# Softplus of two scan chunks at once: the dt of one chunk five units sooner, of the other eight

## The chip, the cores and the metric

The kernel runs on one core of a Trainium2 chip. The metric is the device time of one execution in microseconds (us). The engines are PE (TensorE, matrix products; PEld is its weight load), DVE (VectorE), ACT (ScalarE, activation functions), POOL (GpSimd) and SP (SyncE, which here does nothing but issue transfers between memory and the chip, one after the other). All of them work from lists of instructions in program order and wait for one another by semaphores.

## The reference

The input x has 4 images of 48 x 48 positions and 128 channels. Layer 0 adds a state-space block to it; layer 1 adds attention and then a spectral convolution. Cut to what matters here:

```python
# layer 0, per image: K=4 orders of the L=2304 positions, d=256 channels, N=16 states
xs = stack([x0, x1, x0[..., ::-1], x1[..., ::-1]])        # rows, columns, both backwards
x_dbl = einsum('bkdl,kcd->bkcl', xs, x_proj_w)
dts_r, Bs, Cs = x_dbl[:, :, :8], x_dbl[:, :, 8:24], x_dbl[:, :, 24:]
dt = softplus(einsum('bkrl,kdr->bkdl', dts_r, dt_proj_w) + dt_proj_b)
A = -exp(A_logs)
for l in range(L):                                        # a scan along the positions
    h = h * exp(dt[l] * A) + (dt[l] * xs[l]) * B[l]
    ys[l] = sum_n(h * C[l])
x = x + out_proj(layernorm(ys of the 4 orders added) * silu(z))
# layer 1
t = t + softmax(ln(t) ln(t)^T) ln(t)
t = t + spectral_convolution(ln(t))                       # 16 filters, long causal convolutions
```

The two functions of ACT that this document is about are in it: softplus makes dt, and exp(dt A) makes the decay of every state at every position.

## The kernel before

The four images (batches) are worked off in a pipeline. For each batch b there are two stages: the scans of b, with the spectral convolution of batch b - 1 laid between their instructions (in batch 0 a mixing of filters, `mixture`), and then the epilogue and attention of b, with the input projection of batch b + 1 laid between. After the last batch the last convolution runs alone.

**Chunks and units.** A scan is cut into chunks of CS = 384 positions: 4 orders x 6 chunks = 24 chunks a batch, 96 in all (`order`, which lists them by k and c). A chunk's 256 channels and 16 states make 8 units (`quads`: h is the half of the channels, q a quarter of the states), and a unit has four scans of 128 x 384 (L510, on DVE). So a batch has 192 units. Before its scans a unit needs dt x B (L494, on DVE for five units of eight, on POOL for three), and for each scan a decay, exp(A dt), made by ACT (L503). After them POOL multiplies by C (L520) and PE sums over the states (L528).

**The ring.** The decays go to PSUM tiles, a `Ring` of 5 in batch 0 and 4 after it. `fill` has ACT make decays as long as a tile is free, so ACT runs ahead of DVE by what the ring holds. Two other things borrow tiles of the ring: a copy of B for the units that DVE enters (`spread`, L486), and the products of the next chunks' preparation (`mm_hold`).

**Preparation of a chunk.** `Chunk.prep` is a generator that `prepare` calls three times per unit; three calls are a step. It takes 15 steps (`STEPS`) and begins 17 units (`LEAD`) before the chunk's first unit, so two or three chunks are prepared at a time. For k < 2 PE projects x (L407) and ACT writes the result to a tile xd (L412), which SP stores to `xdd` in memory; for k >= 2 SP loads xd from there (L398). Then, for each half h, PE makes dt (L421) and ACT copies it to `re` (L424). ACT applies Softplus to both halves at once (L433). DVE makes dt x (L451), SP stores dt and dt x of each half to memory (L440), and loads them back replicated over partitions as `rep` (L445), four transfers per half. `rep` is what the decays and the units read.

**B and C.** `fetch` (L472) broadcasts rows of `xdd` to the tiles `bc0` to `bc7`, four transfers of SP per tile. In the scans the tiles are fetched again one by one, as they come free. For the first chunk of a batch `begin_scans` fetches all eight, 32 transfers.

**The start of a batch's scans.** `begin_scans` is a generator too. For batch 0 it runs at one go behind the input projection. For the others it is called once per step of attention over its last 23 steps (`BEGIN`); a step of attention is one product for the scores (L811), one Exp on ACT (L813) and one product with the values (L803). It prepares chunk 0 in full, fetches its B and C, and carries chunk 1 through 27 calls. Attention's own work of a step, its tail for a finished block among it (`tail`, whose loads and stores go to SP as well: `tu<-td`, `ud<-uT` at L1052, `td<-T` at L1019), comes in the lists ahead of what `begin_scans` adds in that step. After the last step the scans begin, and with them the convolution `stu`, whose first instructions fetch its table tiles `tt` (L1110).

**The convolution.** `stu` has 5 blocks of output rows x 16 filters = 80 items. An item is three sets of products on PE (L1151), whose results ACT copies (L1167, L1171, L1174, L1175), and a projection (L1214). At a block's first item `begin` loads its inputs, among them the residual `res` (L1187), which `ended` adds to the result one or two items after the block's last.

Of the kernel before, what the change touches and what calls it, by code (L numbers as in the profile page):

```python
# [8 lines left out]
F32 = mybir.dt.float32  # L9
AF = mybir.ActivationFunctionType  # L10
# [49 lines left out]
def hybrid_kernel(ctx: ExitStack, tc: tile.TileContext, a: dict, out: bass.AP):  # L60
# [304 lines left out]
    class Chunk:  # L365


        def __init__(self, b, k, c):
            self.b, self.k, self.lo = b, k, c * CS
            self.name = f"{b}_{k}_{c}"  # L370
            self.bc, self.rep = {}, []
            self.rev = k >= 2
            self.first = c == (NCH - 1 if self.rev else 0)
            self.last = c == (0 if self.rev else NCH - 1)

            self.slot = CS if self.rev else 0
            self.at = slice(0, CS) if self.rev else slice(1, CS + 1)

        def prep(self, pool):

            k, name, xc = self.k, self.name, xcs[self.b]
            xdd_ = xdd[k % 2][self.lo // CS]

            def rest(n=1):

                yield  # L390
                yield 0
                yield
                for i in range(3 * n - 3):
                    yield 0 if i % 3 == 1 else None

            if k >= 2:
# [12 lines left out]
            yield 2 * CS if k < 2 else 0  # L409
            yield  # L410
            if k < 2:
                nc.scalar.activation(xd, ps[:, :CS], AF.Identity, bias=onerow)  # L412
                mm_done(hold)
            yield from rest()

            re = pool.one.tile([P, NH, 2, CS], F32, tag="re", name=f"re{name}")
            for h in range(NH):
                hold = mm_hold()
                yield
                ps = mm_tile(f"dt{name}_{h}", hold)  # L420
                nc.tensor.matmul(ps[:, :CS], dtw[:, k, h * P:(h + 1) * P], xd, start=True, stop=True)  # L421
                yield CS
                yield
                nc.scalar.copy(re[:, h, 0], ps[:, :CS])  # L424
                mm_done(hold)
                if h == 0:
                    if k < 2:
                        nc.sync.dma_start(xdd_, xd)
                    yield from rest()
            yield  # L430
            yield 0

            nc.scalar.activation(re[:, :, 0], re[:, :, 0], AF.Softplus)  # L433
            yield
            yield
            yield 0
            d = dram.tile([NH, G4, DL, 2, CS], F32, tag="dtdu", name=f"dtdud{name}")

            def store(h):
                nc.sync.dma_start(d[h].rearrange("g j i t -> (g j) i t"), re[:, h])  # L440

            def load(h):
                rep = pool.rep.tile([P, G4, 2, CS], F32, tag="rep", name=f"rep{name}_{h}")
                for c in range(C4):
                    nc.sync.dma_start(rep[c::C4], d[h].rearrange("g j i t -> j g i t"))  # L445
                self.rep.append(rep)

            for h in range(NH):
                x = in_order(xc[h], k, self.lo, CS)
                dt, dx = [re[:, h, i].rearrange("p (r w) -> p r w", w=x.shape[2]) for i in range(2)]  # L450
                nc.vector.tensor_tensor(dx, dt, x, ALU.mult)  # L451
# [12 lines left out]
            yield  # L464
# [78 lines left out]
    POOLED = ((0, 3), (1, 1), (1, 3))  # L543
    order = [(k, c) for k in range(K) for c in (range(NCH) if k < 2 else reversed(range(NCH)))]
    quads = [(h, q) for h in range(NH) for q in range(Q4)]
    STEPS = 15
    LEAD = 17
    FETCHED = range(2 * Q4)

    CHUNK_COLS = len(quads) * CS + 3 * CS  # L550

    def begin_scans(b, pool):

        chunks = [Chunk(b, k, c) for k, c in order]
        preps = [ch.prep(pool) for ch in chunks]
        for i in range(7):
            next(preps[0])
        for i in range(3 * STEPS - 7):
            if next(preps[0]) is not None:
                yield  # L560
        for i in FETCHED:
            chunks[0].fetch(i, pool)
        for i in range(3 * (LEAD - len(quads))):
            if next(preps[1]) is not None:
                yield
        for i in range(3 * (LEAD - 2 * len(quads))):
            next(preps[2])
        yield chunks, preps

    def scans(b, chunks, preps, front, sp, back, ring, finish, work, work_cols):  # L570
# [39 lines left out]
        def prepare(s):  # L610

            ci, j = divmod(s, len(quads))
            for c in range(ci + 1, ci + 4):
                if c < len(chunks) and 0 <= s - len(quads) * c + LEAD < STEPS:
                    done[0] += next(preps[c]) or 0

        def refill(s, i):
# [439 lines left out]
    def stu(b, pool, ps, seeds):  # L1057
# [119 lines left out]
        def begin(n):  # L1177
            (lo, hi, place, extra), k = items[n]
            m = 2 if extra else 1

            now["x"] = pool.one.tile([P, 6, P], F32, tag="ux", name=f"ux{b}_{n}")
            nc.sync.dma_start(now["x"][:, 2:, :hi - lo], ud[:, :, 1 + lo:1 + hi])
            nc.sync.dma_start(now["x"][:, :2, :hi - lo], ud[:, 2:, lo:hi])
            now["mu"] = pool.one.tile([P, 2, 3, C], F32, tag="mue", name=f"mue{b}_{n}")
            nc.sync.dma_start(now["mu"][:, :m], mud[:, place:place + m])
            now["T", n] = pool.two.tile([P, 4, C], F32, tag="res", name=f"res{b}_{n}")
            nc.sync.dma_start(now["T", n][:hi - lo], td[4 * lo:4 * hi].rearrange("(p j) c -> p j c", j=4))  # L1187

        def parts(w, extra):
# [56 lines left out]
        for n, (_, k) in enumerate(items):  # L1246
            if k == 0:
                begin(n)
            yield from conv(n, 0)
            if n > 0:  # L1250
                fetch_G(n - 1)
# [279 lines left out]
    run(prologue(0, turn.one, mm_tile), 3, weights(once.one))  # L1531
    turn.close()
    once.close()
    front = Stage(tc, "f0", "left", one=(1, SB), xd=(3, SB), rep=(3, SB))
    first = begun(begin_scans(0, front))
    begin0.close()
    start_y(0)
    for b in range(B):
# [48 lines left out]
                parts.pop(0)()  # L1587
        if more:
            turn.close()
            front = Stage(tc, f"f{b + 1}", "left", one=(1, SB), xd=(3, SB), rep=(3, SB))  # L1590
            start_y(b + 1)
            pieces = begin_scans(b + 1, front)
        first = None
# [81 lines left out]
```

## Time and profile before

| | |
|---|---|
| time, median of 3 runs | 5618.99 us (5607.94 to 5623.74) |
| the profiled execution, its own time | 5605.93 us |
| span of its instructions | 5604.2 us |
| mean granted clock of TensorE | 0.931 |
| scans of batches 0 to 3, first to last scan | 951.4, 1006.6, 1006.6, 1000.0 us |
| what follows the last scan (attention of batch 3, then the last convolution alone) | 788.1 us |

The profile is of one execution. A line of its groups has the line of the kernel, the engine, the operation, the tiles (written <- read), shapes, the count, then busy time, the mean of one in ns, and the idle time of the engine before it. In a timeline a line has the start from the span's start, the length, the engine (SPq is SP's queue of transfers), and in brackets the idle time before it with what ended it. Neighbouring instructions of one kind on one engine are merged, with their count.

### The profile page before, as it was taken

To read this page: it belongs to the slowest core of one execution; us is meant where nothing else is said; L and a number is where in the kernel's file an instruction comes from. 1 tells how busy PE (TensorE), PEld (TensorE's weight loads), DVE (VectorE), ACT (ScalarE), POOL (GpSimd) and SP (SyncE) were. 2 spreads that over 40 slices of the span, in tenths; PEclk is the share of its full clock that TensorE was granted. 3 is DMA by queue.
4 is the path that set the end of the run, shared out by engine and by line. 5 is a ranking of instruction groups with operands and counts; after the bars stand their busy time and mean duration, and the time that the engine had idled before them with its cause. 6 is when DMAs were issued, how large, how long until landed. Compare 5 with 4: busy or idle time off the path is not lost. (4 is left out here: it accounts for less than half of the span.)

```text
span 5604.2 us, 74073 instructions
## 1 busy us (share of the span) xinstructions
PE 4809.4 (86%) x23582; PEld 3073.9 (55%) x23582; DVE 4344.4 (78%) x5307; ACT 3324.7 (59%) x6923; POOL 3661.9 (65%) x1882
## 2 busy tenths in 40 slices
PE   3556556688999998898999998898999999889999
PEld 1211111345556666645566666645666667659987
DVE  6999999855899999756999999656999999523211
ACT  2777777546777776446777776446777766432111
POOL 1899999614889998505888998505888998301100
PEclk6877777799999999999999999999999999999999
DMA  3545545306777778416777878417887778226543
GB/s 104 164 150 169 168 158 168 102 30 180 234 239 251 257 252 266 158 33 200 229 245 244 262 242 280 133 39 206 240 249 251 256 249 281 92 63 158 143 146 94
DMA packets 741422, 1035.17 MB, mean 185 GB/s; under 512 B 142760, under 2 KB 564904, under 8 KB 740968
## 3 DMA queue, kind: packets, MB, share of 16 engines
q1 hardware_dynamic: 735208, 1027.13, 58.5%
q10 hardware_dynamic: 5824, 3.30, 0.3%
q8 instruction: 189, 3.10, 0.2%
q14 instruction: 201, 1.65, 0.1%
HBM read 911.77 MB, written 118.31 MB: 184 GB/s over the span
## 5 line engine op out<-in xcount | busy, mean ns | idle before, releaser
L510 DVE TENSOR_TENSOR_SCAN s<-ring,s 128x385 f32<-128x385 f32 x3072 | 2702.3, 940 | 130.9 <-ACT ring L503 129.8
L520 POOL TENSOR_TENSOR s<-s,bc 128x1536 f32<-128x1536 f32 x764 | 2426.6, 3178 | 127.6 <-DVE s L510 62.7
L503 ACT ACTIVATE ring<-rep,A 128x384 f32<-128x384 f32 x3072 | 1758.6, 584 | 784.5 <-DVE s L494 458.1
L494 POOL TENSOR_TENSOR s<-rep,bc 128x1536 f32<-128x1536 f32 x288 | 994.2, 3452 | 162.5 <-DMA bc<-xdd 161.6
L494 DVE TENSOR_TENSOR s<-rep,ring 128x1536 f32<-128x1536 f32 x480 | 832.0, 1734 | 92.3 <-ACT ring L486 40.9
L528 PE MATMUL y<-s,csum 128*32 128x384 f32 x6144 | 712.0, 538 | 184.0 <-POOL s L520 111.6
L1151 PE MATMUL cx<-tt,us 128*128 128x252 f32 (+7 forms) x2880 | 630.3, 359 | 92.7 <-ACT U L1175 55.5
L1151 PE MATMUL cx<-tt,u 128*128 128x252 f32 (+7 forms) x2880 | 620.9, 356 | 63.4 <-ACT cy L1167 62.1
L1151 PE MATMUL cy<-tt,u 128*128 128x252 f32 (+5 forms) x2880 | 611.6, 354 | 31.0 <-DMA tt<-fd 31.0
L1151 PEld LDWEIGHTS cx<-tt,us 128*128 128x128 f32 x2880 | 484.1, 193 | 273.4 <-issue 88.4
L1151 PEld LDWEIGHTS cx<-tt,u 128*128 128x128 f32 x2880 | 479.8, 192 | 275.2 <-ACT cy L1167 101.5
L1151 PEld LDWEIGHTS cy<-tt,u 128*128 128x128 f32 x2880 | 488.3, 194 | 165.6 <-issue 116.0
L1214 PE MATMUL pr<-U,G 128*128 128x288 f32 (+6 forms) x1536 | 451.2, 423 | 11.6 <-DMA G<-gd 11.5
L528 PEld LDWEIGHTS y<-s,csum 128*32 128x32 f32 x6144 | 126.4, 111 | 544.7 <-issue 273.2
L1468 POOL TENSOR_TENSOR t<-s,s 128x512 f32<-128x512 f32 x48 | 63.7, 1326 | 541.1 <-ACT s L1466 541.1
L813 ACT ACTIVATE e<-s,shift 128x512 f32<-128x512 f32 (+1 forms) x360 | 230.9, 644 | 290.7 <-PE s L811 290.3
L931 PE MATMUL G<-M,W 128*128 128x256 f32 (+3 forms) x512 | 234.9, 574 | 192.1 <-ACT W L921 83.4
L811 PE MATMUL s<-xnT 128*128 128x512 f32 (+1 forms) x720 | 341.3, 559 | 13.3 <-ACT xnT L771 13.3
L803 PE MATMUL o<-e,xn 128*128 128x512 f32 (+1 forms) x720 | 337.4, 552 | 2.1 <-ACT e L813 2.1
L518 POOL COPY carry<-s 128x4 f32<-128x4 f32 x640 | 121.2, 189 | 323.8 <-DVE s L510 288.0
L1214 PEld LDWEIGHTS pr<-U,G 128*128 128x128 f32 x1536 | 256.1, 192 | 138.1 <-issue 81.4
L931 PEld LDWEIGHTS G<-M,W 128*128 128x128 f32 x512 | 102.9, 233 | 320.3 <-issue 131.4
(236 smaller groups left out, 5203.6 us busy)
## 6 DMA issues: line engine op xcount, KB each, us to landing
rep<-dtdud SPq DMA_DIRECT2D x768, 384.0 KB
bc<-xdd SPq DMA_DIRECT2D x3072, 48.0 KB
tt<-fd SPq DMA_DIRECT2D x144, 577.0 KB
dtdud<-re SPq DMA_DIRECT2D x192, 384.0 KB
tt<-fd SPq DMA_DIRECT2D x144, 505.0 KB
tt<-fd SPq DMA_DIRECT2D x144, 379.0 KB
G<-gd SPq DMA_DIRECT2D x160, 256.0 KB
t<-fd SPq DMA_DIRECT2D x80, 384.0 KB
```

Source lines behind the costliest of these rows:

```text
L494: eng.tensor_tensor(s, self.ch.rep[self.h][:, :, 1], bt.unsqueeze(1).to_broadcast([P, G4, CS]), ALU.mult)
L503: nc.scalar.activation(ring.body(self.dA[g]), ch.rep[self.h][:, g, 0], AF.Exp, scale=A[:, ch.k, self.h * G4 + g, self.q:self.q + 1])
L510: nc.vector.tensor_tensor_scan(s, ring.decays(i, ch.rev), s, 0.0, ALU.mult, ALU.add)
L518: nc.gpsimd.tensor_copy(carry[:, self.h, self.q].unsqueeze(2), self.s[:, :, end:end + 1])
L520: eng.tensor_tensor(self.s, self.s, ch.bc[Q4 + self.q].unsqueeze(1).to_broadcast([P, G4, CS]), ALU.mult)
L528: nc.tensor.matmul(ch.y[g * DL:(g + 1) * DL, :CS], csum, self.s[:, g], start=(self.q == 0), stop=(self.q == Q4 - 1))
L803: nc.tensor.matmul(po[J][:, :w], xn[:, i], e[:, :w], start=(i == 0), stop=(i == NT - 1))
L811: nc.tensor.matmul(p[:, :w], xnT[:, i * P:(i + 1) * P], xnT[:, 512 * J:512 * J + w], start=True, stop=True)
L813: nc.scalar.activation(e[:, :w], p[:, :w], AF.Exp, bias=shift)
L931: nc.tensor.matmul(p[:, :n], W[:, q if t else 0, i], M[t][:, i].unsqueeze(1).to_broadcast([P, n, C]), start=(t == 0 and i == 0), stop=(t = ...
L1151: nc.tensor.matmul(p4[:, 1:3, v - (hi - at):] if g else p4[:, 0:4:3, v - (hi - at):], x, t[:, :, hi - 1 - at + J * P:end if end >= 0 else ...
L1214: nc.tensor.matmul(o if q else o.rearrange("p f r m -> p r f m"), G, U[n][:, 4 * q:4 * q + 4, v0:v1].rearrange("p (a b) m -> p a b m", a=2 ...
```

## The change

The preparation of even and odd chunks (by their place in `order`) gets different lengths. An even chunk begins 5 units sooner and waits 5 steps between its copies of dt and its Softplus, so that its Softplus stays where it was. An odd chunk begins 8 units sooner and waits 8 steps behind its Softplus, so that everything from dt x on stays where it was. The Softplus of chunk c + 1 thereby comes in the same call of `prepare` as that of chunk c, right behind it. As dt now lives longer, `re` becomes three tiles: `dt0` and `dt1` for even and odd chunks, and `dx` for dt x; a half of a chunk is stored with two transfers in place of one. To make room, `xd` has two buffers in place of three, and the residual of the convolution one in place of two; it is loaded at the second to last item of its block. `begin_scans` prepares chunks 0 and 1 side by side up to their Softplus, then the rest of chunk 0 together with the first 18 calls of chunk 2, and then fetches B and C.

```diff
+            self.odd = i % 2
...
-            re = pool.one.tile([P, NH, 2, CS], F32, tag="re", name=f"re{name}")
+            dt = pool.one.tile([P, NH, CS], F32, tag=f"dt{self.odd}", name=f"dt{name}")
...
-            nc.scalar.activation(re[:, :, 0], re[:, :, 0], AF.Softplus)
+            if not self.odd:
+                yield from rest(EARLY)
+            nc.scalar.activation(dt, dt, AF.Softplus)
+            if self.odd:
+                yield from rest(len(quads))
             yield
             yield
             yield 0
+            dx = pool.one.tile([P, NH, CS], F32, tag="dx", name=f"dx{name}")
...
             def store(h):
-                nc.sync.dma_start(d[h].rearrange("g j i t -> (g j) i t"), re[:, h])
+                for i, x in enumerate((dt, dx)):
+                    nc.sync.dma_start(d[h].rearrange("g j i t -> (g j) i t")[:, i], x[:, h])
...
-    STEPS = 15
-    LEAD = 17
+    EARLY = 5
+    STEPS = (15 + EARLY, 15 + len(quads))
+    LEAD = (17 + EARLY, 17 + len(quads))
...
-        for i in range(7):
-            next(preps[0])
-        for i in range(3 * STEPS - 7):
-            if next(preps[0]) is not None:
+        calls = [0] * len(preps)
+
+        def go(c, n):
+            for i in range(calls[c], n):
+                next(preps[c])
+            calls[c] = n
+
+        DT = 23
+        for i in range(8, DT + 4):
+            go(0, min(i, DT))
+            go(1, i - 3)
+            if i % 3 != 0:
+                yield
+        go(0, DT + 3 * EARLY)
+        go(0, DT + 3 * EARLY + 1)
+        go(1, DT + 1)
+        ends = [3 * (LEAD[c % 2] - len(quads) * c) for c in range(4)]
+        ends[0] = 3 * STEPS[0]
+        yield
+        for i in range(DT + 3 * EARLY + 2, ends[0] + 1):
+            go(0, i)
+            go(2, min(i - DT - 3 * EARLY, ends[2]))
+            if i % 3 == 0:
                 yield
         for i in FETCHED:
             chunks[0].fetch(i, pool)
-        for i in range(3 * (LEAD - len(quads))):
-            if next(preps[1]) is not None:
-                yield
-        for i in range(3 * (LEAD - 2 * len(quads))):
-            next(preps[2])
+        for c in range(1, 4):
+            go(c, ends[c])
         yield chunks, preps
...
-            for c in range(ci + 1, ci + 4):
-                if c < len(chunks) and 0 <= s - len(quads) * c + LEAD < STEPS:
+            for c in range(ci + 1, ci + 5):
+                if c < len(chunks) and 0 <= s - len(quads) * c + LEAD[c % 2] < STEPS[c % 2]:
                     done[0] += next(preps[c]) or 0
...
-            now["T", n] = pool.two.tile([P, 4, C], F32, tag="res", name=f"res{b}_{n}")
+
+        def residual(n):
+            (lo, hi, place, extra), k = items[n]
+            now["T", n] = pool.one.tile([P, 4, C], F32, tag="res", name=f"res{b}_{n}")
...
+            if k == KF - 2:
+                residual(n - k)
...
-    front = Stage(tc, "f0", "left", one=(1, SB), xd=(3, SB), rep=(3, SB))
+    front = Stage(tc, "f0", "left", one=(1, SB), xd=(2, SB), rep=(3, SB))
```

The last edit stands a second time, for the batches after the first.

More of the change, by code (lines that the diff above doesn't have):

```diff
@@ L365, in hybrid_kernel, with __init__ @@
     class Chunk:
-        def __init__(self, b, k, c):
+        def __init__(self, b, i, k, c):
             self.b, self.k, self.lo = b, k, c * CS
+            self.odd = i % 2
             self.name = f"{b}_{k}_{c}"
@@ L423, in prep @@
                 yield
-                nc.scalar.copy(re[:, h, 0], ps[:, :CS])
+                nc.scalar.copy(dt[:, h], ps[:, :CS])
                 mm_done(hold)
@@ L449, in prep @@
                 x = in_order(xc[h], k, self.lo, CS)
-                dt, dx = [re[:, h, i].rearrange("p (r w) -> p r w", w=x.shape[2]) for i in range(2)]
-                nc.vector.tensor_tensor(dx, dt, x, ALU.mult)
+                v, o = [y[:, h].rearrange("p (r w) -> p r w", w=x.shape[2]) for y in (dt, dx)]
+                nc.vector.tensor_tensor(o, v, x, ALU.mult)
             yield
@@ L552, in begin_scans @@
     def begin_scans(b, pool):
-        chunks = [Chunk(b, k, c) for k, c in order]
+        chunks = [Chunk(b, i, k, c) for i, (k, c) in enumerate(order)]
         preps = [ch.prep(pool) for ch in chunks]
-        for i in range(7):
-            next(preps[0])
-        for i in range(3 * STEPS - 7):
-            if next(preps[0]) is not None:
+        calls = [0] * len(preps)
[19 more added lines that the diff above has]
+            if i % 3 == 0:
                 yield
@@ L1589, in hybrid_kernel @@
             turn.close()
-            front = Stage(tc, f"f{b + 1}", "left", one=(1, SB), xd=(3, SB), rep=(3, SB))
+            front = Stage(tc, f"f{b + 1}", "left", one=(1, SB), xd=(2, SB), rep=(3, SB))
             start_y(b + 1)
```

## The prediction

> **What bounds the kernel now.** I read the page's first part first (busy time of each engine, share of the span, instructions):
>
> ```profile
> PE 4809.4 (86%) x23582; PEld 3073.9 (55%) x23582; DVE 4344.4 (78%) x5307; ACT 3324.7 (59%) x6923; POOL 3661.9 (65%) x1882
> ```
>
> ACT, whose work the change regroups, is the least busy of the five. The change lives in the scans, so the whole-span shares are not the figure to use. L510's instructions fall into four stretches: 119.0 to 1070.3 us (batch 0), 1318.0 to 2324.6, 2566.8 to 3573.4 and 3816.1 to 4816.1 (batches 1 to 3): 3964.5 us of the span. The table of windows, for 140 us inside batch 1 (length, then busy us of PE, PEld, DVE, ACT, POOL, then clock, DMA share, GB/s):
>
> ```profile
> 1680.00:1820.00 140.00, 134.10 (x706) 89.60 (x708) 135.93 (x145) 103.54 (x220) 131.21 (x63) 0.99 0.80 252
> ```
>
> DVE is busy 97%, PE 96%, ACT 74%. DVE is the engine to count on: it loses time only when it sits idle, and it can't make lost time good. Its idle time over the four stretches is 40.8, 76.9, 76.4 and 71.8 us.
>
> What the change goes for is in the groups of ACT and in the waits:
>
> ```profile
> L433 ACT ACT_TABLE_LOAD x95 | 121.9, 1283 | 1.7
> L503 ACT ACT_TABLE_LOAD x89 | 114.2, 1283 | 1.6
> L433 ACT ACTIVATE re<-re 128x768 f32<-128x768 f32 x96 | 81.0, 844 | 1.1
> ...
> DVE s L510 <- ACT ring L503: 129.8, 121, 9.1
> ```
>
> Each of the 96 Softplus has a table load of 1.283 us before it and, before the next Exp, another. The last line is DVE's scans waiting for an Exp: 129.8 us in all. In time it looks like this (start, length):
>
> ```profile
> 3034.17 1.28 ACT L433 ACT_TABLE_LOAD   x1
> ...
> 3035.46 0.84 ACT L433 ACTIVATE re<-re 128x768 f32<-128x768 f32 x1
> ...
> 3036.32 1.28 ACT L503 ACT_TABLE_LOAD   x1
> 3037.62 1.59 ACT L503 ACTIVATE ring<-rep,A 128x384 f32<-128x384 f32 x3
> 3038.24 1.81 DVE L510 TENSOR_TENSOR_SCAN s<-ring,s 128x385 f32<-128x385 f32 x2 [1.37 <-ACT ring L503]
> ```
>
> ACT makes no Exp for 3.44 us; DVE lives on the decays that stand ready in the ring for 2 us and then waits 1.37 us. I read this idle time after each of the 88 Softplus that lie inside the scans: 5.9, 26.9, 25.9 and 27.4 us in the four batches, 86 us of the 129.8.
>
> The start of a batch's scans is the other place (batch 1; in batches 2 and 3 the same waits are 6.8 and 7.1 us where this one ends in 7.39):
>
> ```profile
> 1304.20 0.58 ACT L1050 COPY uT<-utr 128x512 f32<-128x512 f32 x1
> ...
> 1294.72 21.24 SPq L472 DMA_DIRECT2D bc<-xdd  x32
> ...
> 1316.68 0.56 SPq L1052 DMA_DIRECT2D ud<-uT  x1
> 1317.33 0.59 SPq L1019 DMA_DIRECT2D td<-T  x1
> ...
> 1318.01 4.26 SPq L1110 DMA_DIRECT2D tt<-fd  x4
> ...
> 1324.46 2.05 PE L1151 MATMUL cx<-tt,us 128*128 128x252 f32 x4 [10.32 <-DMA tt<-fd]
> 1326.55 0.56 ACT L1167 COPY cy<-cx 128x504 f32<-128x504 f32 x1 [6.29 <-PE cx L1151]
> ...
> 1330.44 1.75 DVE L494 TENSOR_TENSOR s<-rep,ring 128x1536 f32<-128x1536 f32 x1 [7.39 <-ACT ring L486]
> ```
>
> SP spends 21.24 us issuing 32 broadcasts of B and C (0.66 us each). The store of uT, ready at 1304.8, is issued at 1316.7: it stands behind them. So do the first table tiles tt of the spectral part. PE waits for tt, ACT's copy of PE's result waits for PE, the Exps behind that copy wait with it, and DVE waits 7.39 us for ACT. SP's list is what sets this start.
>
> **The skill.** The Trainium skill, "ScalarE: Activation LUTs", What ACT_TABLE_LOAD costs, gives 1283 ns for a load and 1380 ns of drain with it. The trace agrees on the load and shows no drain: Softplus starts 0.01 us after the load, which starts 0.02 us after the copy before it. The same page, Table sets: the hidden batching unit, advises grouping by table set, which is this change. "DMA: Bandwidth & Descriptors", Issuing engines are not separate DMA queues, calls the time to initiate a DMA "usually small relative to the DMA itself". At this start it is not: 21.24 us of issuing for 32 x 48 KB.
>
> **The change, part by part.**
>
> *Softplus in pairs.* Chunks c (even) and c+1 run theirs in the same call of prepare, in that order, with nothing of ACT between. An even chunk keeps its place in the scans; an odd one's moves eight units forward. Loads fall by 96: 123 us of ACT's time, which has room. What counts is DVE. The odd chunks' stalls go: 1.6 us in batch 0, 12.9, 12.8 and 12.9 us in the others. The pair's outage is 3.44 + 0.84 = 4.28 us (an estimate, two rows of the trace added), so an even chunk's stall grows by 0.84 us wherever it is already above zero: 30 places in batches 1 to 3, 25.2 us, and 6 in batch 0, 5.0 us. Where it is zero (3 and 5 places) I take half: 1.3 and 2.1 us. Sum: batches 1 to 3, -38.6 + 25.2 + 1.3 = -12.1 us; batch 0, -1.6 + 5.0 + 2.1 = +5.5 us. Net -6.6 us. Bounds: if the second Softplus costs DVE nothing, -40.2; if the longer outage leaves ACT's backlog of copies to cost another 0.6 us in each of the 44 pairs, +20.
>
> *The start of batches 1 to 3.* begin_scans hands out its work over the last 23 steps of attention. Before, chunk 0 is through after the 14th and its 32 broadcasts follow at once; chunk 1 comes after. Now both are prepared side by side, the Softplus pair is in step 14 (counting the first as 1), chunk 0's stores in 16, its loads in 19 and 21, and the broadcasts in 22, after attention's own step. In SP's list they now stand behind the store of uT, which attention issues in step 22. That store needs ACT's copy of uT: 1304.2 to 1304.8 us before, and later now, because chunk 1's second dt product (0.81 us) and chunk 2's first two products (1.45 + 0.81 us) come ahead of it on PE, which is full there (a step is two products of 0.86 us); one product less stands between, so about 1307. With the store's 0.56 us the broadcasts start at 1307.8, not 1294.7, and end 21.2 us later at 1329.0. Before, three small DMAs stood between them and tt (1.95 us); now one does (td, 0.7 us). tt is issued at 1329.8 against 1318.0: 11.8 us late, and with the same 12.4 us from there to DVE's next instruction, DVE resumes 11.8 us late. It does its first four scans before that, as now, so the delay is idle time of DVE. Three batches: +35.4 us. Bounds: if only chunk 0's loads hold the broadcasts back (from 1302.3), 7.6 us each; if the two extra stores and busier DMA queues add, 14.
>
> *The start of batch 0.* Nothing hides it. Two xp products (1.65 us) and two dt products (1.5 us) of chunk 1 go ahead of chunk 0's last on PE, and one more copy (0.48 us) ahead of Softplus on ACT: the product dt*x, now at 101.0, comes at about 105; with two more stores (0.3 us) chunk 0's loads move from 104.0 to 108.2. The first unit needs the first broadcast, issued behind those loads:
>
> ```profile
> 109.36 22.24 SPq L472 DMA_DIRECT2D bc<-xdd  x32
> ...
> 116.67 0.48 ACT L486 COPY ring<-bc 128x384 f32<-128x384 f32 x1 [9.95 <-DMA bc<-xdd]
> ```
>
> so the scans start +4.2 us.
>
> *At nothing.* Two more stores per chunk: 192 issues of 0.32 to 0.51 us; a chunk's 42 us of SP hold 32 broadcasts (21 us), 8 loads (5 us) and a few others, so 1 us is covered; without cover it would be 96 us, the price of a full SP. dt and x are multiplied in tiles of their own, the same 0.5 us. The third xd buffer goes: an xd tile is read for about 6 units and its buffer comes round after 16. One residual buffer: it is loaded two items (some 25 us) before it is needed and the tile before it is stored by then. dt copies of even chunks come five units sooner and take a ring slot there instead: the same number of slots, other units. DVE's ring waits away from any Softplus are 35 us in batches 1 to 3, so I allow 5 us either way a batch.
>
> **Sum.** 35.4 + 4.2 - 6.6 = +33.0 us on the profiled 5605.9 us (span 5604.2): 5638.9. That run is at the low end of the timed ones (5607.9 to 5623.7, median 5619.0), so I add the difference to the median: 5652 us.
>
> **Rivals.** *The saving scales instead of being capped* (same). Outages cost 86 us of DVE's idle time for 88 x 3.44 = 303 us of ACT, 28%. If the 114 us less outage (44 pairs x 2.60) return 28%, that is 32 us, and with the starts' 39.6 the kernel is at +8: 5627. For it: the stalls do follow Softplus. Against: they begin only once 2 us of ready decays are used up, so a longer outage is paid in full.
> *PE is the true bound in batches 1 to 3* (faster). PE is 96% busy and waits 101.5 us for ACT's cy copies; if each outage delays that chain by its length, three batches save 33 pairs x 2.60 = 86 us, less 40: 5573. It decides once more than 35% of the outage comes back (40 of 114). Against: PE is idle only 12.5 us in the 8 us after the Softplus of a batch, half of what DVE is.
> *The broadcasts are late but DVE is not*: if tt's landing doesn't hold ACT, the starts cost 4 and the scans give 7, 5616 (same). Against: the chain tt, cx, cy, ring stands in the trace.
> *SP runs full* (slower): the added stores and later starts push tt behind in steady work too, +50 us and more over the forecast's end.
>
> **How the numbers follow.** A difference of 0.3% (17 us) is about what a measurement of this kernel can tell. Forecast 0.63, own range 5636 to 5672; scaling 0.11; late but harmless 0.04; PE 0.12; SP full 0.10. Slower is the forecast and the full SP, 0.73; same 0.11 + 0.04 = 0.15; faster 0.12. Range for 8 in 10: 5606 (most of the same cases) to 5678 (starts at 14 us each, scans at +20).
>
> **What would show it.** Table loads near 95 in all; pairs of Softplus 0.84 us apart; DVE's waits for L503 near 120 us, in half as many places, each longer. At a batch's start, bc x32 beginning near 1308 and ending near 1329, tt after it, the wait of ACT's cy copy near 18 us in place of 6.3, DVE's near 17 to 19 in place of 7.4. Wrong, if tt is issued within 3 us of where it was, or if DVE's idle time in mid-scan falls by more than 25 us a batch.

## The result and the profile after

| | before | after |
|---|---|---|
| time, median of 4 runs each | 5621.36 us (5607.94 to 5625.68) | 5652.17 us (5641.33 to 5654.65) |
| ratio, 95% interval | | 1.0059 [1.0046, 1.0072] |
| span of the profiled execution | 5604.2 us | 5650.8 us |
| its own time | 5605.9 us | 5652.5 us |
| mean granted clock of TensorE | 0.931 | 0.927 |
| up to the first scan of batch 0 | 120.5 us | 123.4 us |
| scans of batch 0, first to last | 949.8 us | 950.2 us |
| scans of batches 1, 2, 3 together | 3008.4 us | 3045.2 us |
| the three attention stages between | 737.2 us | 737.0 us |
| after the last scan | 788.2 us | 795.0 us |

The kernel became 0.6% slower, some 31 us by the medians. The ratio's interval reaches from 26 to 40 us. The two profiled executions lie 46.6 us apart. Of that, 6.8 us come after the last scan, where the change has only the later load of the residual. The profiled executions of all the other kernels show 794.7 to 799.0 us there, those built on the kernel before among them, so it was the profile of before that was low. What the change did is in the scans of batches 1 to 3.

(The stretches of scans are counted here from the first scan that DVE ran; the prediction's begin 1.6 us earlier.)

The first part of the page after, busy time of each engine:

```profile
PE 4817.5 (85%) x23582; PEld 3073.7 (54%) x23582; DVE 4328.7 (77%) x5307; ACT 3209.4 (57%) x6829; POOL 3661.1 (65%) x1882
```

ACT was relieved of 115 us, as intended, and DVE has no more to do than before (4328.7 against 4344.4 us). What was added is idle time. In the table of windows, the same 140 us inside batch 1:

```profile
1680.00:1820.00 140.00, 135.23 (x710) 89.88 (x710) 137.52 (x146) 102.79 (x221) 131.13 (x64) 1.00 0.80 248
```

In this stretch DVE is busier than before (137.52 against 135.93 us): the loss isn't spread evenly over the scans. Chunk by chunk (32 scans each, counted from 0, batches 1 to 3 added up) it stands in three places: chunk 0 takes 33.7 us more than before, chunk 12 14.3 and chunk 20 17.2. The other 21 together take 28.4 us less. The groups of ACT, and then two lines of the list of waits (engine, tile, line, what it waited for: us in all, times, longest):

```profile
L436 ACT ACT_TABLE_LOAD x48 | 61.6, 1283 | 0.9
L510 ACT ACT_TABLE_LOAD x45 | 57.7, 1283 | 0.8
```

```profile
DVE s L517 <- ACT ring L510: 197.3, 124, 16.4
ACT cy L1191 <- PE cx L1175: 177.0, 121, 17.3
```

The loads are halved (97 in all, 191 before). Yet DVE's waits for a decay rose from 129.8 to 197.3 us, and the longest went from 9.1 to 16.4 us. ACT's copy `cy` waits 177.0 us for PE where it waited 93.1. The longest of both are at the starts of the scans. The timeline at batch 1's start:

```profile
1306.67 0.54 SPq L1076 DMA_DIRECT2D ud<-uT  x1
1307.32 20.31 SPq L479 DMA_DIRECT2D bc<-xdd  x32
...
1328.36 4.34 SPq L1134 DMA_DIRECT2D tt<-fd  x4
...
1333.79 2.06 PE L1175 MATMUL cx<-tt,us 128*128 128x252 f32 x4 [19.23 <-DMA tt<-fd]
...
1335.88 0.56 ACT L1191 COPY cy<-cx 128x504 f32<-128x504 f32 x1 [15.25 <-PE cx L1175]
...
1336.98 0.96 DVE L517 TENSOR_TENSOR_SCAN s<-ring,s 128x385 f32<-128x385 f32 x1 [14.40 <-ACT ring L510]
```

This is the chain of the prediction: the broadcasts stand behind the store of uT, the tables behind the broadcasts, then PE, ACT and DVE follow. DVE waits 14.40, 16.4 and 14.3 us at the three starts. From the first scan of the batch to the 33rd it takes 64.4, 68.1 and 64.4 us; before it was 54.4 us each time.

A pair in the middle of batch 2, from the timeline:

```profile
3051.20 1.28 ACT L436 ACT_TABLE_LOAD   x1
...
3052.49 1.58 ACT L436 ACTIVATE dt<-dt 128x768 f32<-128x768 f32 x2
...
3054.09 1.28 ACT L510 ACT_TABLE_LOAD   x1
3055.38 1.59 ACT L510 ACTIVATE ring<-rep,A 128x384 f32<-128x384 f32 x3
3056.00 1.81 DVE L517 TENSOR_TENSOR_SCAN s<-ring,s 128x385 f32<-128x385 f32 x2 [0.99 <-ACT ring L510]
```

The outage is 4.17 us (3051.20 to 3055.38, one Exp boundary to the next), against 3.44 us for a single Softplus: the second adds 0.73 us. DVE's idle time, put into classes by where it falls ("right behind" is within 6 us), in batches 1 to 3 together:

| DVE idle, us | before | after |
|---|---|---|
| first 40 us of each batch's scans | 29.0 | 56.2 |
| right behind a Softplus | 80.7 | 67.7 |
| waits for the ring elsewhere | 32.8 | 55.0 |
| waits for PE's y (L540, after it L547) | 24.2 | 49.4 |
| other | 28.9 | 17.0 |
| last 40 us of each batch's scans | 29.6 | 19.9 |

The starts take 27 us more, and behind the Softplus 13 us are saved. But two classes that the prediction left alone grew by 22 and 25 us. So the questions for the runs are: what the late broadcasts cost in time, what the Softplus pair is worth, and what else the change costs.

### The profile page after: what moved, and what is told of

Its sections match the earlier page's. It is cut to its first block, busy times and chain, and to the rows that moved or that the text cites. A ratio compares the mean times of both kernels' runs of the same rounds, so it can differ in the third digit from the quotient of the medians.

```text
span 5650.8 us, 74308 instructions
## 1 busy us (share of the span) xinstructions
PE 4817.5 (85%) x23582; PEld 3073.7 (54%) x23582; DVE 4328.7 (77%) x5307; ACT 3209.4 (57%) x6829; POOL 3661.1 (65%) x1882
## 5 line engine op out<-in xcount | busy, mean ns | idle before, releaser
L517 DVE TENSOR_TENSOR_SCAN s<-ring,s 128x385 f32<-128x385 f32 x3072 | 2696.4, 936 | 197.6 <-ACT ring L510 197.3
L1175 PE MATMUL cy<-tt,u 128*128 128x252 f32 (+5 forms) x2880 | 606.6, 350 | 16.4 <-DMA tt<-fd 16.2
L1175 PEld LDWEIGHTS cy<-tt,u 128*128 128x128 f32 x2880 | 475.9, 190 | 170.8 <-issue 116.2
L525 POOL COPY carry<-s 128x4 f32<-128x4 f32 x640 | 120.5, 188 | 319.9 <-DVE s L517 308.4
```

What stands on the lines that cost most here:

```text
L517: nc.vector.tensor_tensor_scan(s, ring.decays(i, ch.rev), s, 0.0, ALU.mult, ALU.add)
L1175: nc.tensor.matmul(p4[:, 1:3, v - (hi - at):] if g else p4[:, 0:4:3, v - (hi - at):], x, t[:, :, hi - 1 - at + J * P:end if end >= 0 else ...
```

## The experiments

Each ratio is to the kernel before, run on the same chip, with its 95% interval.

### The starts: the broadcasts alone, in both directions

The changed kernel, with the eight tiles of B and C fetched one per step of attention from the seventh step on, so that they are through before chunk 0's loads:

```diff
+        left = list(FETCHED)
         for i in range(8, DT + 4):
...
+            if i >= 17 and i % 3 != 0 and left:
+                chunks[0].fetch(left.pop(0), pool)
...
-        for i in FETCHED:
-            chunks[0].fetch(i, pool)
```

> The changed kernel with one edit: chunk 0's 32 broadcasts of B and C go into SP's list one tile (4 transfers) per step of attention from the seventh step on, in place of all at once in the 22nd. Theory 'SP's list at the start' (three starts of 10.4 us late, 31 of the 33 us): the broadcasts are issued by about 1297, the first table tiles tt by about 1317, and the kernel takes 31 to 37 us less than the changed one, 5615 to 5621 us where before is 5621, so a ratio of 0.998 to 1.001. Rival 'the scans pay' (two more stores per chunk, dt copies in other units, longer outages): the starts recover but the total stays 15 us or more over before, 5636 and up.

Measured: 1.0011 [1.0001, 1.0020], median 5621.2 us. Its timeline at batch 1's start:

```profile
1273.11 2.40 SPq L479 DMA_DIRECT2D bc<-xdd  x4
...
1316.84 4.76 SPq L1137 DMA_DIRECT2D tt<-fd  x4
...
1325.93 0.96 DVE L517 TENSOR_TENSOR_SCAN s<-ring,s 128x385 f32<-128x385 f32 x1 [2.98 <-ACT ring L510]
```

The tables go out at 1316.84 in place of 1328.36, and DVE waits 2.98 us in place of 14.40. The first 33 scans take 54.6, 52.5 and 54.3 us, as before the change. The time falls by 0.48% of 5620 us, 27 us (18 to 36, by the two intervals).

The other direction: the kernel before, with nothing changed but that its broadcasts come behind chunk 1's 27 calls.

```diff
-        for i in FETCHED:
-            chunks[0].fetch(i, pool)
         for i in range(3 * (LEAD - len(quads))):
             if next(preps[1]) is not None:
                 yield
+        for i in FETCHED:
+            chunks[0].fetch(i, pool)
```

> The kernel before with one edit: chunk 0's 32 broadcasts stand behind chunk 1's 27 calls in begin_scans, in the last step of attention. Softplus is not paired and nothing else is changed. Theory 'SP's list at the start': tt is issued about 10 us later in batches 1 to 3, and the kernel takes 28 to 33 us more than before, ratio about 1.0053; batch 0 does not change. Rival 'the scans pay': the delay alone costs under 10 us, ratio under 1.002.

Measured: 1.0042 [1.0027, 1.0058], 24 us (15 to 33), median 5640.4 us.

```profile
1302.08 20.37 SPq L472 DMA_DIRECT2D bc<-xdd  x32
...
1335.02 1.75 DVE L494 TENSOR_TENSOR s<-rep,ring 128x1536 f32<-128x1536 f32 x1 [15.77 <-ACT ring L486]
```

Late broadcasts alone bring DVE's 15.77 us wait (15.2 in the other two batches; 6.8 to 7.4 before) into a kernel with no pair of Softplus in it. Its first 33 scans take 24.5 us more than before in the three batches together. Two runs in opposite directions give 27 and 24 us: this is the larger part of the loss, and shown.

Then the kernel before with early broadcasts, to see whether its own start has something to give:

```diff
+        left = list(FETCHED)
         for i in range(3 * STEPS - 7):
             if next(preps[0]) is not None:
+                if i >= 9 and left:
+                    chunks[0].fetch(left.pop(0), pool)
                 yield
-        for i in FETCHED:
+        for i in left:
             chunks[0].fetch(i, pool)
```

> The kernel before with one edit: chunk 0's broadcasts one tile per step from the time that its xdd is stored. Theory: tt waits for the store of T (ready at 1315.5 in batch 1) and no more for the broadcasts, which gains 1 to 2 us per start, so 3 to 8 us in all and in batch 0 a few us, ratio 0.998 to 1.000. Beside the changed kernel with the same early broadcasts it gives what pairing and its edits are worth by themselves: by the sum of the prediction 6 us in favour of the paired one, by the rival in which the saving scales with the outage 32 us, by 'the scans pay' the paired one is slower.

A miss: 1.0035 [1.0021, 1.0049], slower. The three stretches of attention, 249.2, 243.8 and 244.2 us before, are 258.5, 253.3 and 252.8 us. SP's list at batch 1 shows why:

```profile
1288.91 2.52 SPq L472 DMA_DIRECT2D bc<-xdd  x4
1291.53 0.53 SPq L1022 DMA_DIRECT2D td<-T  x1
1295.29 0.33 SPq L1028 DMA_DIRECT2D tu<-td  x1
```

Attention's own store td and load tu, issued at 1284.86 and 1291.66 before, now stand behind broadcasts and chunk 0's stores and loads, and in the trace DVE waits 20.9 us for `tu` in each of the three batches, where it waited about 11. In the changed kernel with early broadcasts the same pair went out at 1286.28 and 1289.38 and attention lost nothing (249.5, 245.4, 244.2 us). An early transfer is not free either: it has to pass between the transfers that attention needs, and here it did in one kernel and not in the other.

### The stores

The kernel before with dt and dt x in two tiles and two stores per half in place of one, as the change has them:

```diff
-            re = pool.one.tile([P, NH, 2, CS], F32, tag="re", name=f"re{name}")
+            dt = pool.one.tile([P, NH, CS], F32, tag="dt", name=f"dt{name}")
...
+            dx = pool.one.tile([P, NH, CS], F32, tag="dx", name=f"dx{name}")
...
-                nc.sync.dma_start(d[h].rearrange("g j i t -> (g j) i t"), re[:, h])
+                for i, x in enumerate((dt, dx)):
+                    nc.sync.dma_start(d[h].rearrange("g j i t -> (g j) i t")[:, i], x[:, h])
```

> The kernel before with one edit: dt and dt*x in two tiles and two stores per half (192 more stores), no other change. In the changed kernel with early broadcasts DVE's waits for the ring away from Softplus rose by 23 us in batches 1 to 3, and its waits for PE's sum y by 24 us. If SP's list (the stores) causes them, this kernel shows them and is 10 to 30 us over before; if the place of the dt products causes them, it shows neither and is within 8 us of before.

Measured: 1.0018 [1.0011, 1.0024], 10 us [6, 13], median 5629.1 us. Not nothing. The pages' lines of SP's queue (packets, MB, share of 16 engines), before and then this run:

```profile
q1 hardware_dynamic: 735208, 1027.13, 58.5%
```

```profile
q1 hardware_dynamic: 762856, 1027.14, 59.8%
```

The same bytes go out in 27,648 packets more. The page's sizes account for it: the packets between 2 and 8 KB fall by 24,576, which is 192 stores x 128 partitions of 2 x 384 x 4 = 3072 bytes, and each becomes two of 1536; the other 3,072 are 16 small ones for each of the 192 added transfers. The Trainium skill, "Perfetto Trace Analysis", DMA Optimizations, says "Small DMAs (< 2KB) have significant per-transfer overhead". A store here is 192 KB as a whole; only its packets, 1536 bytes in place of 3072, come under that figure. If packets are meant, these runs agree in sign, at 10 us in all. The run adds 192 transfers as well as packets, and doesn't tell the price of the one from that of the other. In the trace, PE's waits for the projection's table rise (`pr` for the load of G, 11.5 to 19.7 us in all), DVE's waits for y with them (48.9 to 57.6), and SP's waits for rep's loads before a broadcast from 134.7 to 149.3 us (177.4 in the changed kernel). These lie near the cost; which of them carries it isn't settled.

The counterpart is a kernel that has the lives of dt that the change needs and yet one store per half: dt0, dx and dt1 side by side in one tile, so that dt0 with dx, and dx with dt1, are each one piece. For an odd chunk dt x then comes first in `rep`, and the units and decays read it there (two more lines of the edit).

```diff
-            dt = pool.one.tile([P, NH, CS], F32, tag=f"dt{self.odd}", name=f"dt{name}")
+            re = self.trio[:, :, self.odd:self.odd + 2]
+            dt = re[:, :, self.odd]
...
-            dx = pool.one.tile([P, NH, CS], F32, tag="dx", name=f"dx{name}")
+            dx = re[:, :, 1 - self.odd]
...
-                for i, x in enumerate((dt, dx)):
-                    nc.sync.dma_start(d[h].rearrange("g j i t -> (g j) i t")[:, i], x[:, h])
+                nc.sync.dma_start(d[h].rearrange("g j i t -> (g j) i t"), re[:, h])
...
+        trio = pool.one.tile([P, NH, 3, CS], F32, tag="trio", name=f"trio{b}")
```

On the changed kernel alone, with its late broadcasts:

> The changed kernel with one edit: the three dt tiles side by side in one, so that a half is stored by one transfer (192 stores fewer); EARLY = 5 and the late broadcasts stay. The price of the split stores inside the change itself: in the kernel before it was 10 us (0.18%), with early broadcasts 15 us (EARLY = 8) and 28 us (EARLY = 5). If the parts add, the changed kernel's 1.0059 falls by one of these: to 1.0041 with the first, to 1.001 with the last; the late broadcasts' 27 us must remain over the same kernel with early ones (0.9960), so 1.0008 by that sum. If late broadcasts hide the stores' price, it stays within 0.001 of 1.0059.

Measured: 1.0042 [1.0028, 1.0056], median 5635.4 us: 0.17% (10 us) below the change's 1.0059, though the two intervals overlap and nothing at all isn't excluded. The starts stay as bad (first 33 scans 64.5, 66.2, 64.5 us). With early broadcasts as well:

> The same single stores with EARLY = 5, the changed kernel's own: with early broadcasts the changed kernel was at 1.0011. Theory 'stores': 6 to 12 us less, ratio 0.999 to 1.000, and 5 to 9 us more than with EARLY = 8. If the place of even chunks' dt products doesn't matter, it equals the kernel with EARLY = 8.

Measured: 0.9960 [0.9948, 0.9972], median 5597.4 us, 0.51% (29 us, 20 to 37) below the 1.0011 of early broadcasts with two stores, and more than was expected. The packets are back at 735,208 in the profiles with a single store.

The traces show one place where the changed kernel pays for its two stores, and that is chunk 12. Over batches 1 to 3 the 14.3 us that it takes more than before become 1.5 with a single store; with early broadcasts it is 12.3 us with two stores and none with one. In batch 1, counted from the chunk's first scan, the changed kernel's four stores go out between 7.0 and 10.6 us, and PE waits 3.48 us for the tables `tt`. With early broadcasts and a single store per half the two stores go out between 3.7 and 4.8 us, and PE has no such wait. In the kernel before with two stores chunk 12 takes no longer than before: its 10 us lie elsewhere.

### The Softplus

What all 190 of its table loads are worth: the kernel before with Exp in the place of Softplus, which leaves out the logarithm (dt is not the reference's) and so needs no load.

```diff
-            nc.scalar.activation(re[:, :, 0], re[:, :, 0], AF.Softplus)
+            nc.scalar.activation(re[:, :, 0], re[:, :, 0], AF.Exp)
```

> The kernel before with Exp in place of Softplus (the logarithm is left out, so dt is another number): the same instructions, but no table load in the scans. It measures what all 190 loads cost. Theory 'ready decays cover the outage': ACT's outage falls from 3.44 to 0.84 us, which the ring covers, so DVE's 80.7 us of waits behind Softplus in batches 1 to 3 and 6 in batch 0 go almost wholly, and of that 50 to 85 us reach the end: ratio 0.985 to 0.991. If PE were the true bound in batches 1 to 3 it would be over 100 us, ratio under 0.982; if other waits take the place of these, under 30 us.

Measured: 0.9932 [0.9917, 0.9948], median 5575.6 us: 38 us by the ratio (29 to 47), 41.5 by the medians, less than the 50 to 85 expected. DVE's idle time right behind the activation goes from 86.6 us to 6.6. Two lines of its waits:

```profile
DVE ya L540 <- PE y L528: 66.8, 39, 7.2
DVE s L510 <- ACT ring L503: 60.0, 60, 11.0
```

The waits for decays fell by 69.8 us (129.8 to 60.0), those for PE's y rose by 17.9 (48.9 to 66.8), and in batches 1 to 3 the ring waits elsewhere rose from 32.8 to 48.3 us. So of the 80 us taken away some 33 came back as other waits. Another 29 us came back as work of DVE, in dt x (before, then this run):

```profile
L451 DVE TENSOR_TENSOR re<-re,xc 128x384 f32<-128x384 f32 x192 | 185.2, 1005 | 37.4 <-ACT re L433 37.4
```

```profile
L451 DVE TENSOR_TENSOR re<-re,xc 128x384 f32<-128x384 f32 x192 | 214.1, 1155 | 31.9 <-ACT re L433 31.9
```

In the kernel before, 147 of the 192 take under 0.9 us, and POOL is busy for 1% of that time; 30 take over 1.5 us, and POOL is busy for 78% of theirs. In this run 45 take over 1.5 us. Taking 2.60 us out of each of the 88 outages in the scans is 229 us of ACT's time, and about 40 us, 17 to 18%, reach the end.

The change with the pairs taken apart, the odd Softplus behind its eight steps of waiting:

```diff
-            nc.scalar.activation(dt, dt, AF.Softplus)
             if self.odd:
                 yield from rest(len(quads))
+            nc.scalar.activation(dt, dt, AF.Softplus)
```

> The changed kernel with one edit: an odd chunk's Softplus stands behind its wait of 8 steps in place of ahead of it, so that it comes where it was in the kernel before and the Softplus are not paired; tiles, stores, starts of the preparation and the late broadcasts are those of the changed kernel. Theory: pairing alone is worth 7 us (12 us in batches 1 to 3, minus 5 in batch 0), so about 7 us over the changed kernel, 5659 us, ratio to before 1.0065 to 1.0075; DVE's waits behind the 88 Softplus go back to about 86 us from 77. Rival 'the saving scales': 32 us over the changed one, 5684, ratio 1.011.

Measured: 1.0095 [1.0078, 1.0113], median 5670.8 us, 0.36% above the change. By itself this would say that pairs save 20 us (8 to 33). But in the profiles the scans of batches 1 to 3 take as long with pairs as without (3045.2 and 3045.4 us); the difference lies in batch 0 (950.2 and 957.4) and in the stretches of attention (737.0 and 742.0). And two other things moved with it: the odd Softplus now stands where the next even chunk's products of dt come through, and at a batch's start its two loads come right ahead of the first scans. Its idle time behind Softplus is 36 us a batch, 9 us more than in the kernel before, which has as many. So two more comparisons were made. The first keeps the early broadcasts, begins even chunks 5 units sooner, and prepares odd ones as before:

```diff
-            if self.odd:
-                yield from rest(len(quads))
...
-    STEPS = (15 + EARLY, 15 + len(quads))
-    LEAD = (17 + EARLY, 17 + len(quads))
+    STEPS = (15 + EARLY, 15)
+    LEAD = (17 + EARLY, 17)
```

> The changed kernel with early broadcasts, but odd chunks are prepared as in the kernel before (15 steps, 17 units ahead), so that Softplus is not paired: what is left is that the dt products of even chunks come five units sooner, and the split tiles. If the place of these products in the chunk causes the new waits, they are here too: 20 us or more of waits for y and for the ring away from Softplus, and the kernel is 10 to 25 us over before. If the pair's longer outage causes them, they are not here and the kernel is within 8 us of before.

Measured: 1.0008 [1.0001, 1.0015], median 5621.8 us, against 1.0011 [1.0001, 1.0020] with pairs. It isn't clean either: its idle time behind Softplus is 36 us a batch too, as the even chunks' products of dt stand where they stood in the run before. Still it takes no longer than the pairs, in all or in the scans of batches 1 to 3 (3014.4 us, and 3016.5 with pairs). The second pair of kernels has early broadcasts, single stores, and even chunks 8 units sooner, once with pairs, and once with every odd Softplus but the first of a batch behind its wait:

```diff
+            if self.alone:
+                yield from rest(len(quads))
             nc.scalar.activation(dt, dt, AF.Softplus)
-            if self.odd:
+            if self.odd and not self.alone:
                 yield from rest(len(quads))
```

> The kernel with EARLY = 8 and early broadcasts (ratio 0.9995), with one edit: dt of even chunks, dt*x and dt of odd chunks lie side by side in one tile, so that one transfer stores a half again (192 stores fewer), and the replicated tile of an odd chunk has dt*x first. Theory 'the split stores cost 10 us through SP's list': 6 to 12 us less, 5600 to 5608, ratio 0.997 to 0.9985. Rival 'the 10 us came from something else in that kernel': within 3 us of the split one.

> The kernel with EARLY = 8, early broadcasts and single stores, with one edit: an odd chunk's Softplus (but for chunk 1's) stands behind its wait, so that the Softplus in the scans are single, each right behind dt products of some chunk as in the kernel before. Beside the paired one it prices pairing alone, all else equal. By the sum of the prediction 6 to 10 us more than paired (DVE's waits right behind Softplus 80 to 90 us against 67 in batches 1 to 3); by the rival in which the saving scales, 20 to 32 us more; if other waits take the place of all that pairing saves, within 3 us.

Measured: 0.9968 [0.9956, 0.9980], median 5601.3 us, with pairs, and 0.9967 [0.9954, 0.9980], median 5597.4 us, without. The waits with pairs, and then without:

```profile
DVE s L517 <- ACT ring L510: 134.7, 101, 6.4
...
DVE ya L547 <- PE y L535: 29.5, 26, 3.3
```

```profile
DVE s L520 <- ACT ring L513: 126.4, 130, 2.7
...
DVE ya L550 <- PE y L538: 23.6, 27, 3.2
```

With pairs there are fewer waits (101 against 130), the longest is longer, and the sum isn't smaller. In batches 1 to 3 DVE's idle time behind Softplus is 65.5 us with pairs and 78.2 without, a gain of 12.7; the ring waits elsewhere are 49.2 and 37.2, those for y 21.3 and 15.9, a loss of 17.4. The pairs as such are worth nothing that these runs can tell, some 10 us either way: what DVE doesn't lose behind a Softplus it loses elsewhere.

### How much sooner

Early broadcasts, two stores, and even chunks 8 units sooner in place of 5:

```diff
-    EARLY = 5
+    EARLY = 8
```

> The changed kernel with early broadcasts and EARLY = 8 in place of 5, so that the dt products of even chunks fall into the same units of a chunk as in the kernel before (5th and 7th), a whole chunk sooner; Softplus stays paired at the same unit. Theory 'place of the products': DVE's waits for y and for the ring away from Softplus fall back by 20 to 45 us of the 47 that they rose, and the kernel takes 5585 to 5605 us, ratio 0.994 to 0.998, faster than before. Rival 'the pair's longer outage makes them': they stay and the ratio is 1.000 to 1.002 as with EARLY = 5.

Measured: 0.9995 [0.9986, 1.0005], median 5613.5 us, against 1.0011 for 5 units; with single stores 0.9968 for 8 units and 0.9960 for 5. The intervals overlap both times and the signs differ, so nothing follows for the time. One class of waits does depend on it: DVE's waits for PE's y in batches 1 to 3 are 39 to 51 us in the six kernels with 5 units and 15 to 31 in the three with 8 (24 before). Between this run and the paired kernel with single stores only the tile, its stores and the order in `rep` differ: 0.9995 to 0.9968, 15 us (7 to 24) for the single store.

## Why the prediction was right, and where not

The forecast was 5652.0 us and the median is 5652.17. That is closer than its terms were: one was too large, one was missing.

**The start of batches 1 to 3** was the main term, and its mechanism is shown, step by step:

| batch 1 | predicted | measured |
|---|---|---|
| store of uT issued | about 1307 | 1306.67 |
| broadcasts begin, end | 1307.8, 1329.0 | 1307.32, 1327.63 |
| tables tt issued | 1329.8 | 1328.36 |
| tt later than before | 11.8 us | 10.4 us |
| wait of the cy copy | about 18 us | 15.25 us |
| DVE's wait | 17 to 19 us | 14.40 us |

The first 33 scans became longer by 10.0, 13.7 and 10.0 us, 33.7 us in place of 35.4. In time the late broadcasts are 24 us (put into the kernel before) to 27 us (taken out of the change). By these figures the term was a quarter to a third too large, but their intervals (15 to 33 and 18 to 36 us) leave it open by how much. A smaller delay is shown: tt was 10.4 us late in batch 1 and not 11.8. That DVE makes part of the delay good isn't shown: with late broadcasts alone the first 33 scans grew by 24.5 us and the time by 24.

**The start of batch 0** came 2.9 us later in the two profiles; predicted were 4.2.

**Softplus in pairs.** The reading held, but for one figure (in the outage shown the ready decays last DVE 2.7 us and not 2, from 3034.17 to 3036.87): the outage is 4.17 us (predicted 4.28), the idle time behind Softplus went from 86.6 to 76.6 us, 10.0 less (predicted 6.6 less), and batch 0, where it was said to grow, has 8.9 in place of 5.9 us. What failed is the step from there to the time, where each microsecond behind a Softplus was counted as one of the end. In the kernel with Exp 80 us went and about 40 reached the end, and with pairs against none 12.7 us went and 17.4 came back as other waits. The 6.6 us are too few to be told from the zero that was measured: the intervals leave some 10 us either way.

**At nothing.** This is the step that failed for the two stores: "1 us is covered" counted SP's issues of a chunk and found room. Whether SP had it isn't settled, but the price was 10 us (0.18%) by the run that does this edit alone, and taking it back gave 10, 15 and 29 us in three surroundings. The prediction priced SP's issues alone and left out the packets; which of the two costs the time isn't separated. That dt x takes the same in tiles of its own held (1005 ns in the mean before, 943 after), but it isn't the 0.5 us of the prediction, which is what it takes at the start of batch 0. The rest of that list (the third xd buffer, the single residual buffer, the moved copies) can't be told from nothing in time: the change with early broadcasts carries all of it and both stores, and is at 1.0011 against 1.0018 for the stores alone. It did move the waits: chunk 20, over batches 1 to 3, is 11 to 17 us longer in every kernel with the earlier preparation and at most 5 in the others, while others become shorter. Why it is chunk 20 stays open.

**The sum**, from the runs: 24 to 27 for the late broadcasts, 10 for the stores, and what is left to the measured 33 (0.59% of 5620 us) is -1 to -4, for everything else, the start of batch 0 and the pairs among it. Predicted: 35.4, 0 and 4.2 - 6.6 = -2.4. By these figures the missing 10 us and the 8 to 11 that were too many on the starts made up for each other, so the hit on the median was luck in part. The parts are known to 4 us (the stores) and 9 us (each figure of the starts), so how exactly they did isn't shown.

**One sign was wrong.** DVE's waits for a decay were to be near 120 us in half as many places, and are 197.3 us in 124. Some 45 us are the three starts: before, they stood in another row (L494 waiting for the copy of B), now the first scan is what waits. Another 22 us are the ring waits away from any Softplus, for which "5 us either way a batch" was allowed. In the change with early broadcasts these stay at 55.7 us, so the late starts don't make them; in the paired kernel with single stores they are 49.2, and in the three kernels without pairs about 37, 30 and 23. So they come with the pairs: part of what is saved right behind a Softplus is lost there.

**The rivals.** *The saving scales*: the pairs take 44 x (2 x 3.44 - 4.17) = 119 us from the outages, and at 28% 33 us would have come back. Even with no load at all only 17 to 18% comes back, and with the pairs nothing that shows. *PE is the true bound* needed over 35%; the same run excludes it. (The 101.5 us in it are the row of PE's weight loads; the products themselves wait 62.1 us for `cy`.) *Late but harmless* falls with the first two runs. *SP full*: some of it was right, as an added store has a price although SP issues for only 75% of the scans of batches 1 to 3, but it was 10 us and not 50.

**What stays open.** Three kernels are below the one before, by 0.32 to 0.40% (18 to 23 us): early broadcasts and single stores, with pairs or without. For the two with 8 units the gain lies in the scans of batches 1 to 3 (2989.7 and 2985.3 us against 3008.4), and since one of them has no pairs, it is to be sought in what they share: broadcasts that are through early, dt made up to eight units ahead, and the later load of the residual. Which of these it is wasn't separated. Early broadcasts alone lost 0.35% in the kernel before, by way of attention.

## What to carry to other kernels

Before you move work ahead in a list, write down what else it issues and behind what those transfers will then stand: here a regrouping of ACT's functions changed nothing by itself that could be measured, and the transfers that moved with it cost 24 to 27 us. Where an engine stalls behind a recurring outage, don't count the whole stall as gain; measure the ceiling first by taking the outage away altogether, which here was about 40 us for all of it. And when a tile is split so that its parts can live for different times, lay the parts side by side so that one transfer still covers them.

## What was not expected of the hardware

- 192 stores more, for the same bytes, cost 10 us, with the DMA engines busy for 78 to 80% of the scans of batches 1 to 3 and SP issuing for 75% of them: each packet of 3072 bytes became two, 27,648 packets more in all.
- A second Softplus directly behind the first adds 0.73 us, less than the 0.84 us that one alone takes.
- 190 table loads, 244 us of ACT, are worth about 40 us of time, though DVE, the engine that is busy 97% in mid-batch, was seen to wait 86.6 us right behind them.
